# Fused grid step, attention and MLP in f32: the first batch's grid step put in another order

## The chip, the cores and the metric

The kernel runs on one core of a Trainium2 chip. The time is the device time of one execution in microseconds (us), taken as the median of several runs. TensorE is PE in the profile (PEld its weight loads), VectorE is DVE, ScalarE is ACT, GpSimd is POOL and SyncE is SP; SPq and ACTq are the queues on which SP and ACT issue DMA transfers. All data is f32 unless said otherwise.

## The reference, cut to what matters

Four stages follow one another for 8 batches of a 512 x 512 array: a grid step, an attention block with a feed-forward part, an expert feed-forward part and a low-rank response. The change touches only the first, and the way into the second, for batch 0:

```python
Af = A_grid[None] * f[:, None]
Bf = B_grid[None] * f[:, None]
gradv_Af = _grad(Af[:, 0], 1) + _grad(Af[:, 1], 2)
gradvv_Bf = (_grad2(Bf[:, 0], 1) + _grad2(Bf[:, 1], 2)
             + _grad(_grad(Bf[:, 2], 2), 1) + _grad(_grad(Bf[:, 2], 1), 2))
df = -gradv_Af + gradvv_Bf * 0.5
x = jnp.maximum(f + df * dt[:, None, None], 0.0)
...
x = _ln(x) * (1.0 + scale) + shift      # scale, shift: an embedding of the timestep
q = (x @ Wq + bq) ...                   # attention follows
```

`_grad` is a central difference and `_grad2` a second difference along one axis, with one-sided formulas in the first and last row or column. A has two grids (A0, A1), B three (B0, B1, B2).

## The kernel before, in words

`fused_kernel` calls `grid_stage` (batch 0's grid step and the preparation of the coefficients for all batches), `attention_stage` and `mlp_stage`. A 512 x 512 grid is held as a tile [128, 4, 512]: partition p has the rows 4p to 4p+3, r is the row in it.

**Loads (L303 to L317).** SP's queue loads b1 and a1 in halves, then b0, a0, f (batch 0), b2, then small tables, W_ada, Wq, Wk and biases. POOL loads the coefficients of the first and last rows (ec8, L298) and, behind a gate that waits for f (L322), the edge rows of f for all batches (fe, L325).

**Coefficients.** Four PE matmuls spread ec8 over batches into PSUM (pec), and ACT copies each to ec (L333). DVE forms ca = b1 + a1, cb = b1 - a1, cc = b0 + b1 (ACT scales it by -2, L339), ce = a0 + b0, cg = b0 - a0; ACT halves b2 (L342). A grid term is a coefficient times f, shifted by a row or a column.

**Sums on PE.** `add` issues four matmuls, one for each r, that add a term to the four PSUM accumulators acc[r]; the shift by a row lies in the choice of r and in which columns of the shifted identity zi are the weights. DVE multiplies e, g, c, ga, gb, q by f in this order (from L356 on), and each product is added on PE: e and g (row shifts), c, then ga and gb (column shifts, 513 wide, with one ghost column made from eight products, L378 to L387), and last t, the column difference of q, added twice. `hg` are eight small matmuls that fetch edge columns of b2 from the neighbouring partition, and ACT copies them to hgs (L371).

**Stores.** When q is there, POOL's gate_c (L398) opens, and POOL stores b2, ce, cg, cc, ca, cb to DRAM (coef_q, e, g, c, a, b, L405 to L412). The later batches' grid steps read them, on DVE, inside the attention. POOL then makes small tables from ca, cb, b2 and hgs.

**Edge rows.** DVE works out the first and last row of all 8 batches in 64 partitions (L441 to L495): xe, the new edge rows. It is a chain of some 40 small operations. The edge rows of batch 0 go from xe into x by four transfers, two on SP and two on ACT (`edges`, L507), all edge rows go to DRAM by four on ACT (xed, L520).

**Layer norm.** PE computes the embedding (`embed`, 32 matmuls of 8 columns, L145). DVE forms x = f + dth * acc for r = 0, 3, 1, 2, ACT clips it at zero (L515), DVE takes statistics (L523, L524), POOL the reciprocal root (L532), DVE normalises the four rows (L535) and adds embed's bias (L159).

**Into the attention.** `x1_in` turns x by 16 PE transposes (xtr) and scales and shifts it; then come the first q, k and v blocks (pq, pk, pv). SP's queue, behind the edge rows, loads the mask, gf (f of batch 1), coef_q, the attention bias bt, Wv, coef_e and so on (L588, L719 to L724, L712, L971, L171).

The order is written out by hand: `pin` is `tc.keep_in_program_order`, which keeps an instruction behind all that was written before it for its engine. Where the operands don't conflict, engines run freely against one another; waits are set by the compiler from the tiles that are read and written. The pool "l0" holds the products e, g, c, ga, gb, q, t in the space that the loaded a0 to b1 leave.

Of the kernel before, what the change touches and what calls it, by code (L numbers as in the profile page):

```python
# [11 lines left out]
F32 = mybir.dt.float32  # L12
# [4 lines left out]
ALU = mybir.AluOpType  # L17
# [205 lines left out]
def grid_stage(  # L223
# [26 lines left out]
    def mm(out, lhsT, rhs, start, stop):  # L250
        pin(nc.tensor.matmul(out, lhsT=lhsT, rhs=rhs, start=start, stop=stop))  # L251

    with ExitStack() as ctx:
# [26 lines left out]
        def rows_in(t, src, r=slice(0, R)):  # L280
            nc.sync.dma_start(t[:, r, :], src.rearrange("(p r) j -> p r j", r=R)[:, r, :])

        with tc.tile_pool(name="raw", bufs=1) as rp:
            a0, b0, a1, b1 = (
                rp.tile([P, R, D], F32, name=k) for k in ("a0", "b0", "a1", "b1")
            )

            ec8 = rp.tile([N // NB, 12, W + 2], F32, name="ec8")
            sel8 = rp.tile([N // NB, N // NB, NB], F32, name="sel8")
            pin(nc.gpsimd.memset(ec8, 0.0))  # L290

            def edge_cols(k):
                lo, hi = max(0, W * k - 1), min(D, W * k + W + 1)
                return slice(lo, hi), slice(lo - W * k + 1, hi - W * k + 1)

            for i, k in enumerate(blocks):
                c, u = edge_cols(k)
                pin(nc.gpsimd.dma_start(ec8[2 * i : 2 * i + 2, :, u], a["edge_c"][:, :, c]))  # L298
            pin(
                nc.gpsimd.tensor_copy(  # L300
                    sel8, ident[0 : N // NB, 0 : N // NB, None].to_broadcast([N // NB, N // NB, NB])
                )
            )  # L303

            halves = slice(0, 2), slice(2, 4)
            for h in halves:
                rows_in(b1, a["B"][1], h)
                rows_in(a1, a["A"][1], h)
            rows_in(b0, a["B"][0])
            rows_in(a0, a["A"][0])  # L310
            rows_in(f, a["x"][0])
            rows_in(b2, a["B"][2])
            nc.sync.dma_start(gw, a["c_ghost"].to_broadcast([P, 16]))
            nc.sync.dma_start(dth, a["dt"][None, :].to_broadcast([P, NB]))
            load_wada()
            load_w("Wq", "Wk")
            load_rows()  # L317
            pin(nc.gpsimd.memset(zi, 0.0))
            pin(nc.gpsimd.tensor_copy(zi[:, 0, 1 : P + 1], ident))
            pin(nc.gpsimd.tensor_scalar_mul(zi[:, 1, 1 : P + 1], ident, -1.0))  # L320
            gate = small.tile([P, 1], F32, name="gate_e", tag="gate_e", bufs=1)
            pin(nc.gpsimd.tensor_tensor(gate, f[:, 0, 0:1], f[:, 0, 0:1], ALU.add))  # L322
            for i, k in enumerate(blocks):
                c, u = edge_cols(k)
                pin(nc.gpsimd.dma_start(fe[n * i : n * i + n, :, u], a["edge_f"][:, :, c]))  # L325

            for i in range(4):
                pec = ps.tile([N, 3, W + 2], F32, name=f"pec_{i}", tag="pec", bufs=2)
                mm(
                    pec, sel8.rearrange("q s b -> q (s b)"), ec8[:, 3 * i : 3 * i + 3, :],  # L330
                    True, True,
                )
                pin(nc.scalar.copy(ec[:, 3 * i : 3 * i + 3, :], pec))  # L333

            for h in halves:
                tt(ca[:, h, :], b1[:, h, :], a1[:, h, :], ALU.add)
                tt(cb[:, h, :], b1[:, h, :], a1[:, h, :], ALU.subtract)
            tt(cc, b0, b1, ALU.add)
            pin(nc.scalar.mul(cc, cc, -2.0))  # L339
            tt(ce, a0, b0, ALU.add)  # L340
            tt(cg, b0, a0, ALU.subtract)
            pin(nc.scalar.mul(b2, b2, 0.5))  # L342


        wp = ctx.enter_context(tc.tile_pool(name="l0", bufs=1, reuse_waits="tile"))
        acc = [ps.tile([P, D], F32, name=f"l0_{r}") for r in range(R)]

        def add(rows, side=0, sign=0, first=False, last=False):

            for r in (0, 3, 1, 2):  # L350
                o = r + side
                turn = 1 + o // R if o in (-1, R) else 1
                mm(acc[r], zi[:, sign, turn : turn + P], rows(o % R), first, last)

        e, g, c = (wp.tile([P, R, D], F32, name=k) for k in "egc")
        tt(e, ce, f, ALU.mult)  # L356
        add(lambda r: e[:, r, :], -1, first=True)
        tt(g, cg, f, ALU.mult)
        add(lambda r: g[:, r, :], 1)
        tt(c, cc, f, ALU.mult)  # L360
        add(lambda r: c[:, r, :])

        hg = ps.tile([P, 2, 2, 3], F32, name="hg")
        for i in range(2):
# [4 lines left out]
                )  # L369
        hgs = small.tile([P, 2, 2, 3], F32, name="hgs", tag="hgs", bufs=1)  # L370
        pin(nc.scalar.copy(hgs, hg))  # L371
        ga = wp.tile([P, R, 513], F32, name="ga")
        gb = wp.tile([P, R, 513], F32, name="gb")
        tt(ga[:, :, 1:513], ca, f, ALU.mult)
        tt(gb[:, :, 0:512], cb, f, ALU.mult)
        g8 = small.tile([P, 2, R, 8], F32, name="g_g", tag="g_g", bufs=1)
        for i, (u, v) in enumerate(
            ((ga[:, :, 1:5], gb[:, :, 0:4]), (gb[:, :, 508:512], ga[:, :, 509:513]))  # L378
# [6 lines left out]
                )  # L385
        pin(nc.vector.tensor_reduce(ga[:, :, 0:1], g8[:, 0, :, :], AX.X, ALU.add))
        pin(nc.vector.tensor_reduce(gb[:, :, 512:513], g8[:, 1, :, :], AX.X, ALU.add))  # L387
        add(lambda r: ga[:, r, 0:512])
        add(lambda r: gb[:, r, 1:513])
        q = wp.tile([P, R, 514], F32, name="q")  # L390
        tt(q[:, :, 1:513], b2, f, ALU.mult)
        d = small.tile([P, R, 2], F32, name="q_d", tag="q_d", bufs=1)
        tt(d, q[:, :, 1:513:511], q[:, :, 2:512:509], ALU.subtract)
        stt(q[:, :, 0:514:513], d, 3.0, q[:, :, 3:511:507], ALU.mult, ALU.add)


        gate = small.tile([P, 1], F32, name="gate_c", tag="gate_e", bufs=1)
        pin(nc.gpsimd.tensor_tensor(gate, q[:, 0, 1:2], q[:, 0, 1:2], ALU.add))  # L398
        coefs = {}
        for m, w, o in (  # L400
            ("q", b2, 1), ("e", ce, 1), ("g", cg, 1), ("c", cc, 0), ("a", ca, 0), ("b", cb, 0)
# [24 lines left out]
        for i, (o, w) in enumerate(((0, (-3.0, 3.0, -1.0)), (509, (1.0, -3.0, 3.0)))):  # L426
            for k in range(3):
                for dst, src in (
# [1 line left out]
                    (gte[:, 0 : R + 2 : R + 1, i, k : k + 1], hgs[:, :, i, k : k + 1]),  # L430
                ):
                    pin(nc.gpsimd.tensor_scalar_mul(dst, src, w[k]))
        t = wp.tile([P, R, D], F32, name="t")
        tt(t, q[:, :, 2:514], q[:, :, 0:512], ALU.subtract)
        add(lambda r: t[:, r, :], -1, sign=1)
        add(lambda r: t[:, r, :], 1, last=True)


        s2 = gp.tile([N, 2], F32, name="s2")
# [50 lines left out]
        tt(se, se, ab[:, 1, 2 : W + 2], ALU.add)  # L490
        tt(se, se, ab[:, 0, C], ALU.subtract)
        tt(se, se, ab[:, 1, C], ALU.subtract)
        xe = cp.tile([N, W], F32, name="xe")
        stt(xe, se, dte, fe[:, 0, C], ALU.mult, ALU.add)
        pin(nc.vector.tensor_scalar(xe, xe, 0.0, None, ALU.max))  # L495
        pe = embed(ps)
        embed_bias()
        pin(nc.vector.tensor_scalar(dth, dth, 0.5, None, ALU.mult))
        st = small.tile([P, R, 6], F32, name="ln0_st", tag="ln0_st", bufs=1)
        mv = small.tile([P, R, 2], F32, name="ln0_mv", tag="ln0_mv", bufs=1)  # L500
        def edges():
# [8 lines left out]
                        )  # L510
                    )

        for r in (0, 3, 1, 2):
            stt(x[:, r, :], acc[r], dth[:, 0:1], f[:, r, :], ALU.mult, ALU.add)
            pin(nc.scalar.activation(x[:, r, :], x[:, r, :], AF.Relu))  # L515
            if r == 3:
                edges()
        xed = dram.tile([n, D], F32, name="xed")
        for i, k in enumerate(blocks):
            pin(nc.scalar.dma_start(xed[:, W * k : W * k + W], xe[n * i : n * i + n, :]))  # L520
# [2 lines left out]
            pin(nc.vector.bn_stats(st[:, r, :], x[:, r, :]))  # L523
            pin(nc.vector.bn_aggr(mv[:, r, :], st[:, r, :]))  # L524

        stats(1)
        stats(2)
        stats(0)
        stats(3)
        rs = small.tile([P, R], F32, name="ln0_r", tag="ln0_r", bufs=1)  # L530
        pin(nc.vector.tensor_scalar(rs, mv[:, :, 1], LN_EPS, None, ALU.add))
        pin(nc.gpsimd.tensor_tensor(rs, rs, mhalf, ALU.pow))  # L532
        for r in range(R):
            pin(
                nc.vector.tensor_scalar(  # L535
                    x[:, r, :], x[:, r, :], mv[:, r, 0:1], rs[:, r : r + 1], ALU.subtract, ALU.mult
                )
            )
        embed_out(pe)

    return dict(coefs=coefs, gab=gab, gte=gte, dth=dth, xed=xed)

# [2 lines left out]
def attention_stage(  # L545
# [13 lines left out]
    with ExitStack() as ctx:  # L559
# [38 lines left out]
            mask_out(b, r)  # L598


        def x1_in(b, c):
            tag, bufs = ("tr", 2) if b or c < 2 else (f"s{c}", 1)
            tr = ps.tile([P, R, P], F32, name=f"xtr_{b}_{c}", tag=tag, bufs=bufs)
            for r in range(R):
                tp(tr[:, r, :], xt[b][:, r, c * P : (c + 1) * P])
            t = io.tile([P, S], F32, name=f"x1_{b}_{c}", tag="x1", bufs=4)
            tv, trv = t.rearrange("f (p r) -> f p r", r=R), tr.rearrange("f r p -> f p r")
            g, h = sc1[:, c, b : b + 1], shift[:, c, b : b + 1]
            if c % 2:
                pin(nc.scalar.activation(tv, trv, AF.Identity, bias=h, scale=g))  # L610
            else:
                pin(nc.vector.tensor_scalar(tv, trv, g, h, ALU.mult, ALU.add))
            x1s[b, c] = t
# [469 lines left out]
        mask_in(0, 1)  # L1083
        load_bias(*units[1])
        load_w("Wo")
        for c in range(KC):
            x1_in(0, c)
        grid_early(0)
        mask_out(0, 0)
        pin(nc.scalar.copy(bvr, bvc[:, :, None].to_broadcast([P, KC, P])))  # L1090
# [871 lines left out]
```

## Time and profile before

| what | value |
|---|---|
| time, median of 3 runs | 2744.86 us (2744.16 to 2745.75) |
| the profiled execution, its own time | 2746.5 us |
| its span | 2744.7 us |
| granted TensorE clock, mean | 0.993 |
| PE busy | 2694.8 us (98%) |
| DVE, ACT, POOL busy | 1906.5, 1034.7, 1501.9 us |
| instructions | 39871 |
| chain that ended last, by engine | PE 93%, DVE 3%, ACT 1%, DMA 1% |

Rows of the view of instructions in time read: start, time, engine, line, operation, what it writes <- what it reads, shape, count, and in brackets the idle time of the engine just before and what ended it. Rows of the chain read: start, time, what. A line such as L245 or L251 is that of a small helper (`tt`, `mm`), so the tile names tell the operations apart. The profiled execution is one run; all the times within it are counted from the start of its span. The grid stage and the way into the attention fill the first 63 us of it.

### The profile page before, as it was taken

What the parts mean: (1) busy time and instruction counts of PE and PEld (TensorE: products, weight loads), DVE (VectorE), ACT (ScalarE), POOL (GpSimd) and SP (SyncE); (2) the same over time, 40 slices, a digit from 0 to 9 for tenths busy, and PEclk for the clock granted to TensorE, in tenths of its full rate; (3) what the DMA queues carried; (4) which work ended last, traced back from release to release, by engine and by line L of the source; (5) the groups of instructions that cost most, each with busy time, mean ns of one, the idle gap of its engine ahead of it and who ended that gap; (6) DMA issues with size and microseconds to landing.
All of it is one profiled execution on the core that took longest, in us unless ns stands there. A gap on an engine that the chain in (4) does not pass through costs nothing.

```text
span 2744.7 us, 39871 instructions
## 1 busy us (share of the span) xinstructions
PE 2694.8 (98%) x14662; PEld 2005.6 (73%) x14662; DVE 1906.5 (69%) x3504; ACT 1034.7 (38%) x2199; POOL 1501.9 (55%) x1091
## 2 busy tenths in 40 slices
PE   7999999999999998999999999999999999999998
PEld 4455555555555555788888888888888888888886
DVE  7888888888888755577666756765456566566565
ACT  2566766667666766211211211211121221221221
POOL 3455555555555653565556655645536636546543
PEclk9999999999999999999999999999999999999999
DMA  8765766666675554642533443253133143142120
GB/s 310 243 214 176 249 192 229 218 201 224 195 242 184 165 162 143 192 128 38 160 127 79 117 144 110 69 168 113 58 127 117 62 152 115 58 158 100 58 77 31
DMA packets 190352, 405.27 MB, mean 148 GB/s; under 512 B 24040, under 2 KB 28720, under 8 KB 183886
## 3 DMA queue, kind: packets, MB, share of 16 engines
q1 hardware_dynamic: 186346, 391.97, 42.9%
q0 software_dynamic: 3360, 10.68, 3.1%
q8 instruction: 117, 1.92, 0.3%
q14 instruction: 77, 0.63, 0.1%
q10 hardware_dynamic: 452, 0.07, 0.0%
HBM read 366.97 MB, written 31.50 MB: 145 GB/s over the span
## 4 chain that ended last, share of the span: by engine, by line
PE 93%; DVE 3%; ACT 1%; DMA 1%; issue 0%; SPq 0%; ACTq 0%; POOL 0%; DVEq 0%
PE u L1173 28%; PE y L1173 28%; PE tr L570 8%; PE s L567 5%; PE ctx L567 4%; PE pq L567 4%; PE pv L567 4%; PE o L567 4%; PE pk L567 3%; PE btr L1176 1%; PE l L251 1%; DVE bt L1005 1%; ACT bt L1010 1%; DVE x L695 1%; PE xb L570 1%; PE ytr L1176 1%
## 5 line engine op out<-in xcount | busy, mean ns | idle before, releaser
L982 POOL TENSOR_TENSOR bt<-bt,mk 128x1024 f32<-128x1024 f32 x256 | 542.4, 2140 | 56.9 <-DMA bt<-in_bias 39.8
L1173 PE MATMUL y<-wo,act 128*128 128x256 f32 x2560 | 572.8, 380 | 0.0
L1173 PEld LDWEIGHTS y<-wo,act 128*128 128x128 f32 x2560 | 481.5, 190 | 69.8 <-issue 6.7
L1010 ACT ACTIVATE bt<-bt,mn 128x512 f32<-128x512 f32 x512 | 365.7, 716 | 78.4 <-DVE mn L1005 77.8
L570 PEld LDWEIGHTS tr<-ident,bt 128*128 128x128 f32 x2048 | 229.4, 141 | 152.9 <-issue 123.2
L1005 DVE CUSTOM_DVE_ANT_0 bt<-s,bt 128x512 f32<-128x512 f32 x512 | 330.7, 683 | 2.4 <-PE s L567 2.4
L1173 PE MATMUL u<-bt,wi 128*128 128x256 f32 x1440 | 330.5, 379 | 0.0
L1179 DVE TENSOR_TENSOR act<-u,u 128x512 f32<-128x512 f32 x256 | 173.1, 686 | 210.0 <-PE u L1173 132.6
L1173 PEld LDWEIGHTS u<-bt,wi 128*128 128x128 f32 x1440 | 273.6, 190 | 37.1
L570 PE MATMUL tr<-ident,bt 128*128 128x128 f32 x2048 | 276.6, 278 | 10.7 <-ACT pt L1033 7.8
L1173 PE MATMUL u<-tb,ws 128*128 128x256 f32 x1024 | 242.2, 379 | 0.0
L1033 ACT COPY pt<-tr 128x512 f32<-128x512 f32 x315 | 177.1, 581 | 163.7 <-PE tr L570 160.1
L1173 PE MATMUL y<-t,s 128*128 128x256 f32 x1024 | 234.2, 380 | 0.0
L1031 DVE COPY pt<-tr 128x512 f32<-128x512 f32 x197 | 135.6, 688 | 115.2 <-PE tr L570 100.5
L1182 POOL TENSOR_TENSOR t<-wo,t 128x512 f32<-128x512 f32 x64 | 105.0, 1656 | 200.5 <-PE y L1173 200.5
L1173 PEld LDWEIGHTS u<-tb,ws 128*128 128x128 f32 x1024 | 194.3, 190 | 26.6 <-DVE tb L1179 0.2
L1173 PEld LDWEIGHTS y<-t,s 128*128 128x128 f32 x1024 | 191.1, 190 | 24.1
L1493 ACT ACTIVATE act<-act,b 128x512 f32<-128x512 f32 x128 | 82.9, 712 | 292.9 <-DVE act L1179 292.9
L1493 ACT ACTIVATE act<-act,bi 128x512 f32<-128x512 f32 x128 | 83.8, 712 | 282.6 <-DVE act L1179 282.6
L1179 DVE TENSOR_TENSOR x<-y,x 128x512 f32<-128x512 f32 (+1 forms) x97 | 64.6, 680 | 158.1 <-PE y L1173 104.2
L1179 DVE TENSOR_TENSOR u<-u,u 128x512 f32<-128x512 f32 x192 | 131.1, 683 | 58.3 <-PE u L1173 58.2
L567 PE MATMUL s<-kt,qt 32*128 32x512 f32 x1024 | 168.1, 645 | 2.5 <-DVE mn L1005 1.6
(327 smaller groups left out, 4253.6 us busy)
## 6 DMA issues: line engine op xcount, KB each, us to landing
bt<-in_bias SPq DMA_DIRECT2D x256, 512.0 KB
wo<-in_W SPq DMA_DIRECT2D x32, 1024.0 KB
wi<-in_Wi SPq DMA_DIRECT2D x32, 1024.0 KB
wo<-in_Wo_e SPq DMA_DIRECT2D x32, 1024.0 KB
wi<-in_W SPq DMA_DIRECT2D x28, 1024.0 KB
gq<-coef_q SPq DMA_DIRECT2D x21, 512.0 KB
x1d<-x SPq DMA_DIRECT2D x8, 1024.0 KB
x<-x1d SPq DMA_DIRECT2D x8, 1024.0 KB
```

Of the source, the lines that this page charges most:

```text
L567: pin(nc.tensor.matmul(out, lhsT=lhsT, rhs=rhs, start=start, stop=stop))
L570: pin(nc.tensor.transpose(out, src, ident))
L982: nc.gpsimd.tensor_tensor(bt, bt, mask[b, r][:, None, :].to_broadcast([P, 2, S]), ALU.add)
L1005: nc.vector.tensor_tensor_reduce(bt[:, i, :], ss[h], bt[:, i, :], -1.0, 3.0e38, ALU.add, ALU.min, mn)
L1010: nc.scalar.activation(bt[:, i, :], bt[:, i, :], AF.Exp, bias=mn, scale=-1.0, accum_out=sums[b, c, r][:, h : h + 1],)
L1031: pin(nc.vector.tensor_copy(pt[:, :, r % 2, :], tr))
L1033: pin(nc.scalar.copy(pt[:, :, r % 2, :], tr))
L1173: pin(nc.tensor.matmul(out, lhsT=lhsT, rhs=rhs, start=start, stop=stop))
L1176: pin(nc.tensor.transpose(out, src, idn))
L1179: pin(nc.vector.tensor_tensor(out, x, y, op))
L1182: pin(nc.gpsimd.tensor_tensor(out, x, y, op))
L1493: nc.scalar.activation(acts[g][:, k, :], acts[g][:, k, :], func, bias=bi[:, j : j + 1])
```

## The change

The first batch's front is put in another order, with fewer tiles for its products:

- The loads: b0 and a0 in halves first, then f, b2, b1, a1 whole.
- ce and cg are formed first; their products with f (written over a0, and into ga's space as vg) are added first.
- Then q = b2 * f, its ghosts, and its difference (into a0), added twice.
- The four pec matmuls and their ACT copies, which stood ahead of the sums, follow here (`edge_coefs`).
- Then cc with its scaling on ACT, ca, the product of cc and f (into b0), cb, hg, and the products ga and gb. Their sums take 511 columns; the two ghost columns are added apart, by matmuls of one column, last.
- POOL's gate_c waits for gb, not for q. gb has q's tile.
- `embed` stands ahead of the edge work in the code, after the last sums on PE as before.
- The x rows 0 and 3 are formed ahead of the last two operations of xe, the edge transfers come after xe, then x rows 1 and 2.
- The reciprocal root is taken for rows 1, 2 and for rows 0, 3 apart, its epsilon added on POOL; embed's bias is added between the two.
- `x1_in` is called twice, for rows 1, 2 of all four blocks and then for rows 0, 3, which also scales and shifts.

```diff
+            ga, q = (wp.tile([P, R, 514], F32, name=k) for k in ("ga", "q"))
+            vg, gb = ga[:, :, 0:D], q
...
             for h in halves:
-                rows_in(b1, a["B"][1], h)
-                rows_in(a1, a["A"][1], h)
-            rows_in(b0, a["B"][0])
-            rows_in(a0, a["A"][0])
+                rows_in(b0, a["B"][0], h)
+                rows_in(a0, a["A"][0], h)
             rows_in(f, a["x"][0])
             rows_in(b2, a["B"][2])
+            rows_in(b1, a["B"][1])
+            rows_in(a1, a["A"][1])
...
+            def add(rows, side=0, sign=0, first=False, last=False, cols=slice(0, D)):
+                for r in (0, 3, 1, 2):
+                    o = r + side
+                    turn = 1 + o // R if o in (-1, R) else 1
+                    mm(acc[r][:, cols], zi[:, sign, turn : turn + P], rows(o % R), first, last)
             for h in halves:
-                tt(ca[:, h, :], b1[:, h, :], a1[:, h, :], ALU.add)
-                tt(cb[:, h, :], b1[:, h, :], a1[:, h, :], ALU.subtract)
+                tt(ce[:, h, :], a0[:, h, :], b0[:, h, :], ALU.add)
+            tt(cg, b0, a0, ALU.subtract)
+            tt(a0, ce, f, ALU.mult)
+            add(lambda r: a0[:, r, :], -1, first=True)
+            tt(vg, cg, f, ALU.mult)
+            add(lambda r: vg[:, r, :], 1)
+            pin(nc.scalar.mul(b2, b2, 0.5))
+            tt(q[:, :, 1:513], b2, f, ALU.mult)
+            d = small.tile([P, R, 2], F32, name="q_d", tag="q_d", bufs=1)
+            tt(d, q[:, :, 1:513:511], q[:, :, 2:512:509], ALU.subtract)
+            stt(q[:, :, 0:514:513], d, 3.0, q[:, :, 3:511:507], ALU.mult, ALU.add)
+            tt(a0, q[:, :, 2:514], q[:, :, 0:512], ALU.subtract)
+            add(lambda r: a0[:, r, :], -1, sign=1)
+            add(lambda r: a0[:, r, :], 1)
+            edge_coefs()
             tt(cc, b0, b1, ALU.add)
             pin(nc.scalar.mul(cc, cc, -2.0))
-            tt(ce, a0, b0, ALU.add)
-            tt(cg, b0, a0, ALU.subtract)
-            pin(nc.scalar.mul(b2, b2, 0.5))
...
-        tt(e, ce, f, ALU.mult)
-        add(lambda r: e[:, r, :], -1, first=True)
-        tt(g, cg, f, ALU.mult)
-        add(lambda r: g[:, r, :], 1)
-        tt(c, cc, f, ALU.mult)
-        add(lambda r: c[:, r, :])
+            tt(ca, b1, a1, ALU.add)
+            tt(b0, cc, f, ALU.mult)
+            add(lambda r: b0[:, r, :])
+            tt(cb, b1, a1, ALU.subtract)
...
         tt(ga[:, :, 1:513], ca, f, ALU.mult)
+        add(lambda r: ga[:, r, 1:512], cols=slice(1, D))
         tt(gb[:, :, 0:512], cb, f, ALU.mult)
+        add(lambda r: gb[:, r, 1:512], cols=slice(0, D - 1))
...
-        add(lambda r: ga[:, r, 0:512])
-        add(lambda r: gb[:, r, 1:513])
-        q = wp.tile([P, R, 514], F32, name="q")
-        tt(q[:, :, 1:513], b2, f, ALU.mult)
...
+        add(lambda r: ga[:, r, 0:1], cols=slice(0, 1))
+        add(lambda r: gb[:, r, 512:513], cols=slice(D - 1, D), last=True)
...
-        pin(nc.gpsimd.tensor_tensor(gate, q[:, 0, 1:2], q[:, 0, 1:2], ALU.add))
+        pin(nc.gpsimd.tensor_tensor(gate, gb[:, 0, 1:2], gb[:, 0, 1:2], ALU.add))
...
-        tt(t, q[:, :, 2:514], q[:, :, 0:512], ALU.subtract)
-        add(lambda r: t[:, r, :], -1, sign=1)
-        add(lambda r: t[:, r, :], 1, last=True)
+        pe = embed(ps)
...
+        embed_bias()
+        pin(nc.vector.tensor_scalar(dth, dth, 0.5, None, ALU.mult))
+        new_rows(0, 3)
         xe = cp.tile([N, W], F32, name="xe")
...
+        edges()
+        new_rows(1, 2)
...
+        for pair in (slice(1, 3), slice(0, 4, 3)):
+            rows = range(R)[pair]
+            for r in rows:
+                stats(r)
+            pin(nc.gpsimd.tensor_scalar(rs[:, pair], mv[:, pair, 1], LN_EPS, None, ALU.add))
+            pin(nc.gpsimd.tensor_tensor(rs[:, pair], rs[:, pair], mhalf[:, 0:2], ALU.pow))
+            if pair.start:
+                embed_out(pe)
+        for r in (1, 2, 0, 3):
...
-        for c in range(KC):
-            x1_in(0, c)
+        for rows in ((1, 2), (0, 3)):
+            for c in range(KC):
+                x1_in(0, c, rows)
```

## Prediction: what the change does to the time

> **What bounds the kernel now.** The page first: TensorE (PE) is busy 98% of 2744.7 us and carries 93% of the chain that ended last, so after the front there is almost no idle time to win or to hide in: what the front gains or loses in reaching the first attention matmuls goes through to the end. Of the chain I therefore read only the front (start us, length us, what):
>
> ```profile
> 23.04 13.34 PE l L251 x24
> 36.37 0.79 PE hg L251 x8
> 37.16 12.14 PE l L251 x28
> ...
> 49.33 0.76 DVE x L248
> ...
> 54.25 5.73 DMA xed<-xe
> ...
> 63.13 9.94 DMA x<-coef_e
> ```
>
> The reader is to see two stretches. To 50.84 us PE's sums of the grid terms set the pace: VectorE (DVE) has everything ready and waits 1.14 us for PE before it forms x. Behind that, a row of loads on SP's queue sets it: it starts behind the edge rows (xe to x), passes the transfers of xe to DRAM (xed), and ends with coef_e, for which DVE sits idle 5.4 us. Next the instructions of the front in order of time, the rows that I cost the change with:
>
> ```profile
> 14.97 0.48 ACT L333 COPY ec<-pec 64x390 f32<-64x390 f32 x1 [4.49 <-PE pec L251]
> 18.87 0.48 ACT L333 COPY ec<-pec 64x390 f32<-64x390 f32 x1 [0.82 <-PE pec L251]
> 19.25 1.91 ACT L339 ACTIVATE cc<-cc 128x2048 f32<-128x2048 f32 x1
> 23.04 6.47 PE L251 MATMUL l<-e,zi 128*128 128x512 f32 x8 [4.20 <-DVE e L245]
> 29.34 3.60 PE L251 MATMUL l<-g,zi 128*128 128x512 f32 x8
> 29.41 2.28 DVE L245 TENSOR_TENSOR gb<-cb,f 128x2048 f32<-128x2048 f32 x1
> 37.16 0.20 DVE L441 TENSOR_REDUCE s<-ident 64x2 f32<-64x64 f32 x1
> 46.59 0.34 DVE L248 SCALAR_TENSOR_TENSOR xe<-se,dte,fe 64x128 f32<-64x128 f32 x1
> 48.47 3.33 DVE L248 SCALAR_TENSOR_TENSOR x<-l,dth,f 128x512 f32<-128x512 f32 x4 [1.14 <-PE l L251]
> 50.84 8.97 PE L145 MATMUL pe<-sc,wada 128*128 128x8 f32 x64
> 59.66 3.47 PE L570 MATMUL xtr<-ident,x 128*128 128x128 f32 x16
> 62.97 3.60 PE L567 MATMUL pq<-x,Wq 128*128 128x512 f32 x8
> ```
>
> A matmul in f32 is two records, so one "add" of four rows is 8 records: 6.30 us for the first (23.04 to 29.34), 3.44 us for each later one (29.34 to 32.78). A DVE operation on a whole grid takes 2.2 us from start to start. The edge rows (37.16 to 46.59) take DVE 9.43 us, now under PE's sums. And ScalarE (ACT) keeps its order: cc was ready at 15.9 (13.61 + 2.29), yet its scaling began at 19.25, right behind the last copy of pec.
>
> **The change, part by part.** *Earlier start.* DVE needs only b0, a0 and f for the first term. Halves land as b1 and a1 did (second half used from 10.87), f as the third megabyte, where b0 landed (13.6). So ce's second half at 10.87, cg 12.0, ce*f 14.2, cg*f 16.4, and PE starts at 16.7 instead of 23.04: 6.4 us won on PE. Free under this: b2 lands where a0 did (16.05), its scaling (1.90) is done at 18.0, before q needs it at 18.6; POOL's gate on f and the loads of fe move up with f; b1 and a1 land by 21.1 (as b2 did) for cc at 25.2.
>
> *The first add.* On the row it costs 6.30 us, because PE runs at half rate until about 28.5, 5.5 us after its start. The Trainium skill (TensorE: Matmul & The Clock Gate, "What you observe" and "What's actually happening") has the full clock after some 3.4 to 4 us of sustained work, with a window that runs free of the kernel. By that, 3.44 + 1.7 to 2.0 = 5.1 to 5.4 us, an estimate; by the row 6.3. I take the row, since the start is as cold; by the rule all below comes 0.9 to 1.2 us earlier.
>
> *Differences of B2 in the middle.* q*f, its ghosts and the difference are ready to run at 21.4, but the difference is written into a0, which PE reads until 23.0: DVE waits 1.6 us. Then difference 23.0, cc 25.2, ca 27.4 to 29.6. PE meanwhile: first add 16.7 to 23.0, cg term to 26.4, the two difference adds to 33.3.
>
> *The copies of pec, moved.* This decides. The four pec matmuls now stand on PE behind those two adds: 33.3 to 35.9 (two records of 390 columns each, at full clock about 0.65 us together, scaled from 0.43 us for one of 512). Their copies stand on ACT ahead of cc's scaling, and ACT holds its order. The last copy starts at 36.0, the scaling at 36.4, and takes 1.9: 38.3. The edge work, which reads the copies, comes far later on DVE and costs nothing by them. On DVE b0 = cc*f waits for that, with cb, the two column terms, their ghosts, all the edge work and the x rows queued behind it. DVE, which finished ca at 29.6, idles 8.7 us, and PE from 35.9 to 40.8.
>
> *From there on DVE sets the end.* b0 38.35, cb, ga, gb (4 x 2.2) to 47.2, ghosts 0.6, edge work 9.43, two small operations 0.2: first x row at 57.45 against 48.47. PE gets c at 40.8, at half rate after 4.9 us idle (after the 1.96 us before 93.38 the windows give a clock of 0.50 until 96.5): 3.44 + 1.8 to 2.8, hg 0.8, two adds 6.9, then 8 ghost-column matmuls of one column, 16 records at about 0.12 (hg: 8 in 0.95), 1.9 us. Sums complete at about 56.2, still under DVE. Splitting off the columns thus costs nothing; without DVE as cover it costs 1.9.
>
> *Tail.* embed's 64 records follow the ghost columns: 56.2 + 9 to 9.7 = about 66. DVE: rows 0 and 3 to 58.9, xe to 59.4, rows 1 and 2 to 60.8; ACT issues two edge transfers first (2.0, as at 50.77), then clips rows 1 and 2 to 62.8. Statistics of rows 1 and 2 end at 63.9, but the next DVE instruction, adding embed's bias, waits for PE until 66, with the statistics of rows 0 and 3 (1.6) behind it; POOL's two operations 1.4 (pow alone was 1.05, a small one 0.2 to 0.3), normalising rows 0 and 3 to 70.1 (60.1 before). Half the transposes lie ahead of that (1.7 us saved); the rest end at 71.8, so pq starts at 71.85 instead of 62.97: +8.9.
>
> *Queues.* The edge transfers on SP wait for xe: 59.45 against 49.91, with mask, gf, coefficients, bias and Wv behind. The xed transfers on ACT go last at 63.1 against 54.25: +8.85 to the chain of loads. POOL's stores of the coefficients are now gated by gb (47.1) instead of q (34.5): first issue 47.8 against 35.2, last landing at about 65.5 against 52.9 (40.26 + 12.6). Before, loads began at 52.4 as the stores ended; now they begin at 61.9 and 3.6 us overlap. At most that is 3.6 us; at least nothing, since before SP's chain left the DMA engines 0.58 and 0.32 busy from 58 to 62. I take 0.7, nearer that row. coef_e lands then at 82.6: +9.5.
>
> *Ghost columns while PE reads the neighbours.* DVE writes column 0 of ga and 512 of gb while PE may still read the other columns of the tile. Rows of x are not held by one another before (the edge transfer at 49.91 goes with row 0 clipped, row 3 not yet), no row shows columns. I take nothing; at worst the edge work waits for the gb add, ended about 54.3, so that x starts 6.3 us later. There is no gain in either.
>
> Sum: PE's way +8.9, the loads' way +9.5; before, PE waits for the second (1.96 us at 93.38 for qt), so it decides, and later stretches have nothing to absorb it. The profiled execution took 2746.5 us, 1.8 outside its span and 1.6 over the median. I put +9.4 on the median 2744.86: 2754.3.
>
> **Rivals.** (A) *cc isn't held.* If cc's scaling ran as soon as cc is there (27.4 to 29.3), DVE would go on and PE's work would set the end: start -6.4, pec matmuls now in its path +2.6, columns +1.9, half the transposes ahead of the last normalising -1.6: -3.5, so 2741.4, not slower. It decides from the point where the scaling ends by 29.6. PE's 1.14 us lead over DVE at 48.47 speaks for PE as bound; ACT's order at 19.25 speaks against. 13%. (B) *Columns hold DVE*: +9.4 + 6.3 = +15.7, 2760.6; 8%. (C) *Stores and loads collide in full*: +8.85 + 3.6 = +12.5, 2757.3; DMA at 1.0 share from 37 to 49 speaks for it, the gaps after 58 against; 6%.
>
> **How the numbers follow.** Likeliest 70%, with 2751 to 2757.5 as its own range (first add 1.2 shorter by the rule, embed 1 us less, loads' share 0 to 3.6). Some 3% is for what I don't see. What a measurement can tell from no change is about 0.2%, 5.5 us. Range 2748 to 2761: it takes in B and C and leaves out A and tails. Slower by over 0.2%: 82% (main, B, C, less the main case's tail); within: 14%; faster by more: 4%, the tail of A, whose own sum stays within.
>
> **What would show it.** Right: ACT's cc starting at about 36 behind the last pec copy; DVE idle some 8.7 us before b0 with ACT as releaser; PE starting l at about 16.7; x rows at 57 with DVE, not PE, as the chain; bias addition waiting for pe; pq at about 72. Wrong: cc scaled before 30; the edge work starting only after gb's add (B); coef_e landing over 3 us later than pq moved (C). A clock that rises earlier, or a stretch after 60 us with more slack than the page shows, would shrink it.

## The result, and the profile after

The changed kernel takes 2756.35 us (median of 7 runs, 2754.36 to 2757.2) against 2745.18 us for the kernel before (7 runs beside it): a ratio of 1.004, 95% interval 1.003 to 1.0051, so 11.2 us or 0.4% slower. The sum on record gave +9.4. The profiled execution took 2756.7 us, with a span of 2754.9; that is 10.2 us more than the profiled execution of before (2746.5).

The chain that ended last, in the front of the kernel after (start us, length us, what), in answer to the one shown of before:

```profile
16.42 16.82 PE l L251 x32
33.24 3.08 PE pec L251 x8
...
36.35 0.48 ACT ec L339
36.82 1.82 ACT cc L368
...
38.67 2.30 DVE b L245
...
41.02 6.18 PE l L251 x8
47.20 0.79 PE hg L251 x8
47.99 8.64 PE l L251 x32
56.63 10.76 PE pe L145 x64
...
67.41 0.04 DVE ada L159
...
69.84 3.41 PE xtr L577 x14
73.25 0.16 SPq L982
...
73.96 9.06 DMA x<-coef_e
```

Before, PE ran without a break from 23.04 to 50.84. Now the chain leaves PE in the middle of its sums: from pec to an ACT copy, to the scaling of cc on ACT, to a product on DVE, and only then back to PE. At the end it goes through embed and the transposes (xtr) to SP's queue, which issues the attention bias (L982) behind them, with a wait of 0.2 us, and then coef_e. The rows of the view of instructions in time (each engine's) that stand for those steps:

```profile
16.42 6.52 PE L251 MATMUL l<-a,zi 128*128 128x512 f32 x8 [16.42 <-DVE a L245]
22.78 3.60 PE L251 MATMUL l<-ga,zi 128*128 128x512 f32 x8
22.98 2.29 DVE L245 TENSOR_TENSOR a<-q 128x2048 f32<-128x2048 f32 x1 [1.84 <-PE l L251]
25.18 2.28 DVE L245 TENSOR_TENSOR cc<-b,b 128x2048 f32<-128x2048 f32 x1
36.35 0.48 ACT L339 COPY ec<-pec 64x390 f32<-64x390 f32 x1 [0.36 <-PE pec L251]
36.73 1.91 ACT L368 ACTIVATE cc<-cc 128x2048 f32<-128x2048 f32 x1
38.67 2.29 DVE L245 TENSOR_TENSOR b<-cc,f 128x2048 f32<-128x2048 f32 x1 [8.99 <-ACT cc L368]
47.85 3.67 PE L251 MATMUL l<-ga,zi 128*128 128x511 f32 x8
47.87 0.18 DVE L398 TENSOR_REDUCE ga<-g_g 128x4 f32<-128x32 f32 x1
57.88 1.41 DVE L248 SCALAR_TENSOR_TENSOR x<-l,dth,f 128x512 f32<-128x512 f32 x2
67.41 0.23 DVE L159 TENSOR_TENSOR ada<-pe,bada 128x64 f32<-128x64 f32 x1 [2.82 <-PE pe L145]
73.41 3.64 PE L574 MATMUL pq<-x,Wq 128*128 128x512 f32 x8
83.05 1.23 DVE L706 TENSOR_TENSOR x<-x,gf 128x1024 f32<-128x1024 f32 x1 [5.21 <-DMA x<-coef_e]
103.34 1.98 PE L574 MATMUL pk<-x,Wk 128*128 128x512 f32 x4 [1.48 <-DVE qt L652]
```

And of before, the two rows against which the last two are read:

```profile
73.09 1.23 DVE L695 TENSOR_TENSOR x<-x,gf 128x1024 f32<-128x1024 f32 x1 [5.45 <-DMA x<-coef_e]
93.38 3.67 PE L567 MATMUL pk<-x,Wk 128*128 128x512 f32 x4 [1.96 <-DVE qt L641]
```

The reader is to see six things. PE starts 6.6 us earlier than before, as meant. cc's scaling starts right behind the last pec copy, though cc had been summed by 27.5 (25.18 + 2.28), and DVE waits 8.99 us for it, the longest wait behind the start. The first x row comes at 57.88 instead of 48.47, now with no wait for PE. DVE writes the ghost column of ga (L398) at the very time at which PE reads its neighbours, with no wait. And the two ways into the attention are late alike: the first q block by 10.4 us (62.97 to 73.41), the first use of coef_e by 10.0 (73.09 to 83.05). They meet at the second k block (pk): PE waits there for qt, which DVE forms behind its work on coef_e, 1.96 us before and 1.48 after, so of the two ways the loads' is the later in both, and this block is late by 9.96 us (93.38 to 103.34).

From 300 to 800 us nothing differs: PE is busy 496.08 us before and 496.19 after.

### The profile page after: what moved, and what is told of

Read it like the earlier page. It is cut to its first block, busy times and chain, and to the rows that moved or that the text cites. A ratio compares the mean times of both kernels' runs of the same rounds, so it can differ in the third digit from the quotient of the medians.

```text
span 2754.9 us, 39909 instructions
## 1 busy us (share of the span) xinstructions
PE 2697.9 (98%) x14678; PEld 2008.7 (73%) x14678; DVE 1899.9 (69%) x3502; ACT 1036.1 (38%) x2199; POOL 1500.7 (54%) x1094
## 4 chain that ended last, share of the span: by engine, by line
PE 93%; DVE 3%; ACT 2%; DMA 1%; issue 1%; POOL 0%; SPq 0%; DVEq 0%; ACTq 0%; POOLq 0%
PE u L1185 28%; PE y L1185 28%; PE tr L577 8%; PE s L574 5%; PE ctx L574 4%; PE pq L574 4%; PE o L574 4%; PE pv L574 3%; PE pk L574 3%; PE l L251 1%; PE btr L1188 1%; DVE bt L1016 1%; ACT bt L1021 1%; PE xb L577 1%; PE ytr L1188 1%
```

## The experiments

All against the kernel before, run beside them on the same chip. "q block" and "coef_e" are the starts of the first pq and of the first use of coef_e in each kernel's profiled execution, and "k block" is by how much the second k block, where the two ways meet, starts later than in before (62.97, 73.09 and 93.38 there). The ratio and its interval are formed from all runs and the last column from the medians, so the two can differ by an us or so (e7, e9). One profile stands for each kernel's runs.

| kernel | time us | before beside it | ratio, 95% interval | q block | coef_e | k block | time less before |
|---|---|---|---|---|---|---|---|
| after | 2756.35 | 2745.18 | 1.0040, 1.0030 to 1.0051 | 73.41 | 83.05 | +9.96 | +11.2 |
| e1 | 2747.77 | 2745.12 | 1.0011, 1.0003 to 1.0019 | 65.61 | 73.96 | +1.62 | +2.7 |
| e2 | 2759.80 | 2745.12 | 1.0056, 1.0042 to 1.0069 | 73.50 | 85.47 | +12.39 | +14.7 |
| e3 | 2754.27 | 2745.12 | 1.0032, 1.0020 to 1.0045 | 72.42 | 80.85 | +8.56 | +9.2 |
| e4 | 2754.72 | 2745.12 | 1.0037, 1.0024 to 1.0050 | 73.59 | 83.28 | +10.24 | +9.6 |
| e5 | 2747.37 | 2745.32 | 1.0007, 0.9999 to 1.0015 | 65.95 | 74.16 | +1.22 | +2.1 |
| e6 | 2745.66 | 2745.32 | 1.0004, 0.9995 to 1.0012 | 66.06 | 74.68 | +1.60 | +0.3 |
| e7 | 2744.38 | 2745.32 | 1.0002, 0.9994 to 1.0011 | 62.64 | 68.73 | -1.88 | -0.9 |
| e8 | 2747.40 | 2745.32 | 1.0008, 1.0000 to 1.0016 | 65.65 | 72.36 | +0.95 | +2.1 |
| e9 | 2742.00 | 2745.80 | 0.9991, 0.9984 to 0.9997 | 60.17 | 69.31 | -3.78 | -3.8 |
| e10 | 2755.27 | 2745.80 | 1.0036, 1.0022 to 1.0049 | 70.91 | 82.92 | +9.85 | +9.5 |
| e11 | 2753.75 | 2745.80 | 1.0030, 1.0017 to 1.0042 | 71.97 | 77.37 | +7.94 | +8.0 |
| e12 | 2746.93 | 2745.80 | 1.0004, 0.9995 to 1.0012 | 65.96 | 73.25 | +0.83 | +1.1 |

The time follows the k block within 1.3 us in every kernel but e2 (2.3).

The theory: the loss is ACT's order, which holds cc's scaling behind copies that wait for PE. First rival: the work that the change adds on PE, or other parts of it.

**e1_unhold.** One instruction of ACT moves, nothing else:

```diff
-            edge_coefs()
             tt(cc, b0, b1, ALU.add)
             pin(nc.scalar.mul(cc, cc, -2.0))
+            edge_coefs()
```

> Kernel after, with one ACT instruction moved: cc's scaling stands ahead of the four copies of pec, all else as after. Theory H (the scaling is held behind the copies, which wait for PE): the scaling runs at 27.5, b0 = cc*f at 29.6 with no wait for ACT, the edge work ends at about 48.5, PE's sums at about 49.2, first x row at about 49.2, embed ends at about 60, pq starts at about 66: about 2748, 8 less than after and 3 more than before. Rival P (PE's added work, pec and ghost columns in its path, makes the loss): taking the hold away only turns DVE's wait into a wait for PE, x rows not before 54: 2753.

```profile
26.60 1.91 ACT L367 ACTIVATE cc<-cc 128x2048 f32<-128x2048 f32 x1 [8.68 <-DVE cc L245]
28.68 2.29 DVE L245 TENSOR_TENSOR b<-cc,f 128x2048 f32<-128x2048 f32 x1
33.17 0.48 ACT L339 COPY ec<-pec 64x390 f32<-64x390 f32 x1 [4.66 <-PE pec L251]
47.88 1.41 DVE L248 SCALAR_TENSOR_TENSOR x<-l,dth,f 128x512 f32<-128x512 f32 x2
```

The rows are e1's ACT and DVE in time. ACT now waits for cc and scales it at 26.60, b0's product has no wait in brackets, and the x rows come 10.0 us earlier than in after (0.9 of it because a shorter first add lets DVE's difference start at 22.07 instead of 22.98). Of the 11.2 us, 8.5 are gone: theory H, and rival P falls. What remains is 2.7 us. In this trace embed ends at 59.53, no later than in before (59.81), yet the transposes start at 61.99 instead of 59.66, since DVE waits 4.97 us for embed with two rows' statistics behind the wait: the tail (tried in e12 and e5).

**e4_hold_in_before.** The hold alone, put into the kernel before: the loop of the pec matmuls and the scaling of cc go behind g's sum (ec8 and sel8 stay longer for it, and t is written over e to make the room).

```diff
         tt(g, cg, f, ALU.mult)
         add(lambda r: g[:, r, :], 1)
+        for i in range(4):
...
+            mm(
+                pec, sel8.rearrange("q s b -> q (s b)"), ec8[:, 3 * i : 3 * i + 3, :],
+                True, True,
+            )
+            pin(nc.scalar.copy(ec[:, 3 * i : 3 * i + 3, :], pec))
+        pin(nc.scalar.mul(cc, cc, -2.0))
         tt(c, cc, f, ALU.mult)
```

> Kernel before, with the hold alone: the four pec matmuls stand behind the sum of g on PE and their ACT copies ahead of cc's scaling; t is written over e to make room, which waits for nothing. Theory H: PE's pec at 32.8 to 35.6, scaling of cc 36.3 to 38.2, c = cc*f at 38.2 instead of 25.0, DVE idle 13 us, edge work to about 62, first x row at about 62 instead of 48.5: 12 to 14 us more than before, about 2758. Rival (the loss of after lies in other parts of the change): within 3 us of before.

```profile
34.64 0.48 ACT L357 COPY ec<-pec 64x390 f32<-64x390 f32 x1 [0.18 <-PE pec L251]
35.02 1.91 ACT L358 ACTIVATE cc<-cc 128x2048 f32<-128x2048 f32 x1
36.96 2.29 DVE L245 TENSOR_TENSOR c<-cc,f 128x2048 f32<-128x2048 f32 x1 [11.84 <-ACT cc L358]
```

The same three rows as in after, in a kernel that has nothing else of the change: a wait of 11.84 us and +9.6 us. The expectation was 12 to 14, with x at 62; x came at 59.48. Of these 2.5 us, 1.2 are a shorter first add (5.06 us instead of 6.30), and 1.1 are DVE's wait for PE ahead of x in before (1.14 us), which the expectation kept and which is gone here.

**e2_embed_early.** embed fills the gap that the hold leaves on PE.

```diff
             edge_coefs()
+            pe = embed(ps)
...
-        pe = embed(ps)
```

> Kernel after, with embed's 32 matmuls moved on PE to just behind pec, where PE sits idle from 36.3 to 41.0 us; the hold on ACT stays. embed then runs at full clock (about 0.1 us a record, 36.3 to 42.8), b0's sum starts 1.8 later but at full clock, x rows stay at 57.9 since DVE sets them, and the bias addition no longer waits for PE (67.4 to about 64.6), so that pq starts about 2 us earlier, at 71.3. Theory L (the chain of loads behind the edge rows, coef_e at 83.0, sets the end): coef_e stays at 83 and the time within 1 us of after, 2755.5 to 2756.5. Rival E (the wait for embed sets it): 2 to 3 us less than after, 2753.7.

A miss for both. embed took 12.15 us (34.77 to 46.92), not 6.5. The stretches of e2, with the granted clock behind POOL's column, show why:

```profile
34.00:36.00 2.00, 2.00 (x14) 1.39 (x14) 0.00 (x0) 1.59 (x3) 0.00 (x0) 1.00 0.00 0
36.00:38.00 2.00, 2.00 (x14) 2.00 (x13) 0.80 (x1) 1.17 (x1) 0.00 (x0) 0.62 0.00 0
38.00:40.00 2.00, 2.00 (x11) 2.00 (x11) 2.00 (x2) 0.00 (x0) 0.00 (x0) 0.50 0.00 0
46.00:48.00 2.00, 2.00 (x8) 1.48 (x8) 1.87 (x13) 0.00 (x0) 1.40 (x4) 0.50 0.07 29
```

PE counts as busy all through, yet the clock falls to half at 36.48, 1.7 us after embed's start at 34.77 and 4.6 after that of pec (31.89). From pec's start to the fall PE has done nothing but pec and embed, small matmuls; that their kind is what lets the clock fall is read from this and from the last section, not tried by itself. b0's sum then starts late and at half rate, x waits 4.71 us for PE, and all behind it, the edge transfers with the loads, is 2.4 us later than in after.

**e3_gate_ca.** The stores' gate on ca instead of gb.

```diff
-        pin(nc.gpsimd.tensor_tensor(gate, gb[:, 0, 1:2], gb[:, 0, 1:2], ALU.add))
+        pin(nc.gpsimd.tensor_tensor(gate, ca[:, 0, 1:2], ca[:, 0, 1:2], ALU.add))
```

> Kernel after, with POOL's gate for the stores of the coefficients on ca (there at 29.7) instead of gb (47.6). Stores of q, e and g start at about 30, c waits for cc's scaling (38.6), a and b follow, the last landing before 55 instead of 67. DVE's hold stays. The sum on record gave the collision of stores and loads 0.7: the time falls by 0.5 to 1.5, 2755. Rival C (stores and loads collide in full): mask and gf no longer wait for the edge transfers (65.3 falls to about 62), coef_e lands 3.5 us earlier, time 2752.8.

```profile
80.85 1.23 DVE L706 TENSOR_TENSOR x<-x,gf 128x1024 f32<-128x1024 f32 x1 [2.77 <-DMA x<-coef_e]
101.94 1.88 PE L574 MATMUL pk<-x,Wk 128*128 128x512 f32 x4
```

Time 2754.27, 2.1 us less than after, and between the two. coef_e comes 2.2 us earlier, but xe's last step itself started 1.16 earlier (58.42 against 59.58, by a shorter first add): about 1.0 is the stores' own, near the 0.7 on record. The mask did go 4.9 us earlier (60.50 instead of 65.35), as rival C has it, but the loads behind it did not keep that lead. Rival C falls. PE's wait for qt is gone: PE's way is now the later.

**e10_after_bias_last and e11_after_loads_free.** Which of the two late ways sets the end? e10 moves the bias addition of after behind the normalising; e11 frees the loads of after (e3's gate, and SP's two edge transfers on POOL's queue). e10, then e11 without e3's line:

```diff
-            if pair.start:
-                embed_out(pe)
...
+        embed_out(pe)
```

```diff
-                for side, q_ in ((0, nc.sync), (1, nc.scalar)):
+                for side, q_ in ((0, nc.gpsimd), (1, nc.scalar)):
```

> Kernel after, with embed's bias added last on DVE; the hold on ACT stays. DVE no longer waits 2.8 us for embed (67.4), rows 0 and 3 are normalised by about 69.5, pq starts at about 71.5 instead of 73.4; coef_e stays at 83. If PE's way sets the end in after: 1.5 to 2 less than after, 2754.5. If the loads' way does, as the sum on record had it: within 0.5 of after, 2756.

> Kernel after, with the stores' gate on ca (as e3) and SP's two edge transfers on POOL's queue (as e7); hold and bias stay. coef_e lands 4 to 6 us earlier than in after (before 79), pq stays at about 73. If the loads' way sets the end in after: 2 less than e3, 2752. If PE's way does: the same as e3, 2754.

In after the loads' way sets it, by 1.5 us of wait, and behind that PE's. By the times alone neither run settles the question: against the kernel before, e10 stands at +9.5 and after at +11.2, e11 at +8.0 and e3 at +9.2, and in both pairs the intervals overlap for the most part. The traces do. The PE rows of e10:

```profile
70.91 4.13 PE L573 MATMUL pq<-x,Wq 128*128 128x512 f32 x8
81.32 13.97 PE L573 MATMUL pv<-Wv,x 128*128 128x512 f32 x32 [0.92 <-DMA Wv<-in_Wv]
103.23 1.98 PE L573 MATMUL pk<-x,Wk 128*128 128x512 f32 x4 [2.41 <-DVE qt L651]
```

The q block comes 2.5 us earlier than in after (0.8 of it by a shorter first add), coef_e only 0.1, and PE loses the whole lead in waits for Wv and qt: the second k block starts at 103.23 instead of 103.34. That e10's profiled execution was 1.2 us shorter than after's comes from behind the front, where a sum of the attention ran at half clock in after and at full clock in e10 (after's row first):

```profile
152.54 3.25 PE L574 MATMUL ctx<-pt,v 128*32 128x256 f32 x32
151.58 1.93 PE L573 MATMUL ctx<-pt,v 128*32 128x256 f32 x32
```

In e3 and e11 PE waits for qt no longer. coef_e is 3.5 us earlier in e11 than in e3, but the second k block only 0.6 (101.32 against 101.94), about as much as x itself (56.27 against 56.72): once PE's way is the later, freeing the loads brings little.

**e12_tail_in_before, e5_bias_last.** The tail by itself: its part of the diff alone in the kernel before, and e1 with the bias addition moved behind the normalising (the edit of e10). e12's core:

```diff
-        stats(1)
-        stats(2)
-        stats(0)
-        stats(3)
...
+        for pair in (slice(1, 3), slice(0, 4, 3)):
...
+            if pair.start:
+                embed_out(pe)
...
-        embed_out(pe)
...
-        for c in range(KC):
-            x1_in(0, c)
+        for rows in ((1, 2), (0, 3)):
+            for c in range(KC):
+                x1_in(0, c, rows)
```

> Kernel before, with only the tail of the change: statistics, roots and transposes two rows at a time, embed's bias between the pairs. embed ends at 59.66 as before, DVE waits for it from about 56 with the statistics of rows 0 and 3 behind: these end at 61.5, rows 0 and 3 are normalised at 64, pq starts at about 65.5 instead of 63.0: 2 to 2.5 more than before, 2747.5. Rival (half the transposes ahead of the last normalising wins more than the wait costs): 1 less than before, 2744.

> Kernel of e1 (hold undone), with embed's bias added on DVE after the normalising, as in before, instead of between the two pairs of statistics, where DVE waited 5.0 us for embed. If after the hold the wait for embed is what e1 still loses (pq at 65.6 against 63.0, coef_e at 74.0 against 73.1): statistics of rows 0 and 3 run at about 55.5, all rows are normalised by 59.5, the transposes follow embed at 59.6, pq starts at about 63.2: 2745.5, the time of before. Rival (the pairs and the split transposes cost by themselves, or the late stores do): no more than 0.5 less than e1, 2747.5.

```profile
59.95 0.23 DVE L159 TENSOR_TENSOR ada<-pe,bada 128x64 f32<-128x64 f32 x1 [4.83 <-PE pe L145]
62.29 3.84 PE L571 MATMUL xtr<-ident,x 128*128 128x128 f32 x16 [2.37 <-DVE x L537]
65.96 3.60 PE L568 MATMUL pq<-x,Wq 128*128 128x512 f32 x8
```

These are e12's rows. DVE waits 4.83 us for embed with two rows' statistics behind the wait, and the q block is 3.0 us late (2.5 expected). The second k block is late by only 0.83, since before's PE had 1.96 us of wait there to lose; the time rose by 1.1, with an interval that takes in no change. e5 is inconclusive: it gained 0.6 against e1's +2.7, and its profiled execution had a PE that ran at half rate longer (first add 6.37 us, and b0's sum behind pec 5.0), which took back in that execution what the bias had cost. So the traces show the tail's cost in the q block, and how much of e1's 2.7 us it makes up is not settled.

**e6_gate_too, e7_edges_pool, e8_before_edges_pool, e9_ghosts_whole.** Towards a version that beats both. e6 is e5 with e3's gate, e7 adds the edge transfers on POOL's queue, e8 is before with that edit alone, e9 is e7 with the ghost columns summed with their rows again:

```diff
-        add(lambda r: ga[:, r, 1:512], cols=slice(1, D))
-        add(lambda r: gb[:, r, 1:512], cols=slice(0, D - 1))
...
-        add(lambda r: ga[:, r, 0:1], cols=slice(0, 1))
-        add(lambda r: gb[:, r, 512:513], cols=slice(D - 1, D), last=True)
+        add(lambda r: ga[:, r, 0:512])
+        add(lambda r: gb[:, r, 1:513], last=True)
```

> Kernel of e5, with POOL's gate for the stores on ca as in e3: the stores run from 29 to about 48 and are gone when the edge transfers (50) and the loads start. pq stays at about 63, coef_e lands about 1.5 to 2 us earlier than in e5. If the later of the two ways sets the end, nothing more is won than the loads' lag, 0.5: 2745. Rival (stores cost the PE's way too, by the edge rows that land late for the statistics): 1.5 less than e5, 2744.

> Kernel of e6, with the two edge transfers of SP issued on POOL's queue, so that mask, gf, coefficients, bias and Wv are not queued behind xe on SP. If that order is what makes coef_e late in all kernels (DVE idle 2.8 to 5.4 us for it), coef_e lands before 68, DVE no longer waits for it, PE's wait for qt goes: 1 to 2 us less than e6, 2743.5. Rival (the loads' buffers are not free before x is formed, or PE's way sets the end alone): same as e6.

> Kernel before, with that one edit: the two edge transfers of SP on POOL's queue. In before coef_e (73.1) is the later way, with 5.4 us of idle DVE and 2.0 of PE at 93.4 behind it; if the order on SP makes it late, 1.5 to 3 us less than before, 2743. Rival (buffers not free): within 0.5 of before.

> Kernel of e7 (hold undone, bias added last, stores early, edge transfers off SP), with the sums of ga and gb as in before: ghost columns worked out first, then whole rows of 512 columns, so that the 16 records of one column (1.7 us on PE) go. PE still has the c sum to do when DVE writes the ghosts, so it waits for nothing: sums end 1.7 earlier, embed and with it the transposes 1.7 earlier, pq at about 61: 2743, 1.4 less than e7 and about 2 less than before. Rival (x rows are then DVE's, and the layer norm, not embed, sets the transposes): within 0.5 of e7.

e6 and e7 can't be told from before (+0.3 and -0.9), nor from one another: PE's sums end 3.4 us earlier in e7's profile (47.73 against 51.10), which lies before the edge transfers that it moves: the clock was at full for more of the sums. e8 is a miss: 2.1 us slower, with an interval that begins at no change. The edge rows now land late: POOL issues them at 50.28, behind f's transfer of 1 MB at 45.93, which is the likely reason, but no run takes it away. DVE waits 2.65 us for them in its statistics (57.75 instead of 55.10) and SP's gf waits 9.9 us for the same transfers, so that taking SP's queue out of these transfers' way brings nothing by itself. e9 is the best: 2742.0, 0.9991 of before (0.9984 to 0.9997), with PE's sums ended at 46.72 instead of 50.84. By the ratio that is 2.5 us, below the 0.2% of the text above, but its interval does not reach 1. Against e7 it gains more than the 1.4 expected (about 3 us by the ratios), and in the two profiles embed's length is most of it (e7's row, then e9's):

```profile
47.73 11.61 PE L145 MATMUL pe<-sc,wada 128*128 128x8 f32 x64
46.72 9.41 PE L145 MATMUL pe<-sc,wada 128*128 128x8 f32 x64
```

embed runs 2.2 us less when whole rows stand ahead of it instead of one-column records. Over all profiles the two groups don't overlap: 10.88 to 11.81 us in the eight kernels with one-column records ahead of embed, 8.82 to 9.72 in the five without, and 12.30 in e2, where pec stands ahead.

## Why the prediction was right, and where a term was off

*The start of PE* (16.7 on record): 16.42. *The first add* (6.30 by the row, 5.1 to 5.4 by the rule): 6.36 in after. Over all fourteen profiled executions it took 4.90 to 6.54 us, so row and rule are both draws from one spread. That fits what the rule says of a window that runs free of the kernel (the Trainium skill, TensorE: Matmul & The Clock Gate, "What's actually happening"), though the page's spread of 500 ns to either side for the change of clock is narrower than what was found: full clock came 2.81 (e2) to 6.10 us (e6) after PE's first sum began. Taking the row was luck of 1 us.

*DVE's wait before the difference* (1.6): 1.84. *The hold* (cc scaled at 36.4, DVE idle 8.7): 36.73 and 8.99. This step carries the result, and e1 and e4 show it from both sides. *x rows* (57.45): 57.88. *Ghost columns beside PE* (nothing): no wait at 47.87; rival B fell by that row.

One sign of the right case did not come as written: the chain runs over PE's sums and embed to 67.41, not over DVE's x rows, though x had no wait. *embed* was the term mis-sized: on record 9 to 9.7 us from 56.2, ending at 66, after its 8.97 in before. It began at 56.49 and ended at 67.37, having run 10.88 us, of which 7.7 at half clock; no kernel with one-column records ahead of it took less. So *splitting off the columns* did not cost nothing: beside their own 1.7 us under DVE they go with some 2 us more of embed, which DVE waits for. *The q block* (+8.9) therefore came +10.4.

*coef_e* (+9.5): +10.0, of which about 1.0 is the stores' by e3 (0.7 on record). The text let the loads' way decide, and in after it does (e10), with the second k block at +9.96. So embed, though mis-sized, is not what the sum lacks: 9.4 against 9.96 at this block and 10.2 between the two profiled executions. The 11.2 of the medians lies 1.0 above that, within the runs' spread (2754.36 to 2757.2).

Rival A (2741.4, cc not held) was tried as e1: 2747.8. Its mechanism was right and its price wrong: it took half the transposes ahead of the normalising for a gain of 1.6, and left out that embed takes longer (11.39 us in e1) and that the bias addition makes DVE wait for it (4.97 us).

What stays open: how much of e1's 2.7 us the tail is, and what e6 and e7 owe to their edits and what to the clock's draw, since they differ by less than the runs' spread.

## What to carry to other kernels

When a step is moved behind others on one engine, look at its consumers' queues too: the copies of pec were in nobody's way, but on ACT they stood ahead of an instruction that everything else waited for. An early start is worth what the slowest queue lets through: 6.6 us won on PE turned into 9 us of idle DVE. Cheap work in a gap of PE isn't free where it lets the clock fall for the sums behind it (e2). And where two ways are late alike, a single profile's end time can mislead: follow both to the instruction where they meet.

## What the runs showed of the hardware that was not expected

Small matmuls cost the clock though PE counts as busy. In after, from the view of stretches (PE's records in brackets, clock behind POOL's column):

```profile
56.00:58.00 2.00, 2.00 (x20) 2.00 (x19) 1.73 (x10) 0.00 (x0) 2.00 (x9) 1.00 1.04 419
60.00:62.00 2.00, 2.00 (x11) 2.00 (x11) 1.11 (x2) 0.00 (x0) 0.00 (x0) 0.50 1.03 434
```

20 records of embed in 2 us at full clock, 11 at half; the weight loads (second figure) fill the time too. Pec, whose matmuls use 8 rows, does it as well: in e5 b0's sum directly behind pec took 5.0 us instead of 3.44, with no idle time between; in e1 and e7, with the same code for PE up to there, it took 3.54.

The instants at which the clock changed, read from the traces, say when it happens. In each of the fourteen traces they lie whole multiples of 3.41 us apart, on a grid that stands differently to the kernel in each execution:

| kernel | clock to full, half, full, ... at us | apart, in 3.41 us | in the stretch of 3.41 us that ends there |
|---|---|---|---|
| after | 22.16, 35.81, 46.05, 59.70, 73.36 | 4, 3, 4, 4 | to 35.81: pec 2.64 us; to 59.70: embed 3.21 |
| before | 28.68, 55.99, 62.81 | 8, 2 | to 52.57: embed 1.73, no fall; to 55.99: embed 3.41 |
| e2 | 19.41, 36.48, 50.13 | 5, 4 | to 36.48: pec 1.71, embed 1.70 |
| e5 | 22.32, 35.97, 39.39, 53.04 | 4, 1, 4 | to 35.97: pec 2.65 |
| e7 | 19.43, 50.15, 63.81 | 9, 4 | to 33.09: pec 1.23, to 36.50: pec 1.66, no fall; to 50.15: embed 2.42, one-column records 0.99 |

Over all fourteen, up to 64 us, the clock fell from full to half at the end of every such stretch in which pec, embed, one-column records and idle time of PE together took 2.64 us or more, and of none in which they took 1.90 or less; nothing lies between. So the draw is where the grid cuts the small matmuls: in e7 it cuts pec in two, in e5 not. It also fits embed's length, since small matmuls just ahead of it fill the stretch in which it begins, so that the clock falls sooner. What counts for the clock, columns, rows or the gaps between matmuls, these runs do not separate. With the first add's 4.90 to 6.54 us this is some 3 us of spread in one front.
